# Layer 0's second plan when all tokens are counted, the first convolution's loads in the source's order, and one count for layer 1's last plans

## The chip, the cores and the metric

The kernel runs on one core of a Trainium2 chip. The metric is device time in microseconds (us) of the slowest core, which here is the only one. TensorE, VectorE, ScalarE and GpSimd each run one stream of instructions; SyncE (SP) only issues DMAs. Before the change three runs took 1766.63, 1774.96 and 1779.28 us: a median of 1774.96 us.

## The reference, cut to what matters

Two layers work on an image x of shape [2, 256, 56, 56] in float32. Each adds a token mixer on normalised channels, then a mixture of experts (MoE) on normalised tokens:

```python
# layer 0
x = x + local_attention(_ln_c(x))          # 7 x 7 window, 8 heads
t = _to_tokens(x)                          # 6272 tokens of 256
t = t + moe0(_ln_t(t))                     # returns its own input too
# moe0: probs = softmax(tokens @ router.T); top 2, weights made to sum to 1
#   out = tokens + sum_e combine[:, e] * (gelu(tokens @ w1[e] + b1[e]) @ w2[e] + b2[e])
#   8 experts, 256 -> 256 -> 256
# layer 1
x = x + conv_pair(_ln_c(x))
# conv_pair: out1 = relu(bn(tri_conv(x, w1)))
#            relu(out1 + bn(tri_conv(out1, w2)))
# tri_conv: 3 x 3, 256 -> 256, weights made ternary, centre tap counted twice
t = t + moe1(_ln_t(t))                     # top 2 of 8 experts, 256 -> 512 -> 256
```

Batch norm takes its mean and variance over both images, so the second convolution can't start before the first has ended. Nor can an expert's last tokens be known before the last token is routed.

## The kernel before

**Strips.** The image is cut into 14 strips of 8 rows (448 tokens, held as 112 partitions x 4 tokens). Attention, routing, convolution and the final sums go strip by strip.

**Routing** (`routing`). For each strip `settle` takes the two largest router logits of each token with two calls of `first_max` on VectorE, writes which experts were chosen into `hots`, adds them up in `seen`, and finds each token's place within its expert by two small matmuls (`rk`, the rank). Then GpSimd copies the normalised row `u` of each token to its two places in the DRAM buffer `xs`, by indirect DMAs at L861 (one of 112 rows for each of 4 tokens and 2 choices: 8 per strip). `settle` is a generator: each `yield` ends a step, and the caller runs one step of it beside each step of other work. `gates` makes the final weights of the chosen experts (L880 to L893).

**The plan** (`tiles(part)`, L907 to L996). Expert work is cut into tiles of 256 rows of one expert. Which expert and which rows of `xs` a tile has depends on the routing, so a plan is worked out on the chip: a cast of `seen` (L907), a matmul of it with ones (`counts`, L910), and a chain of short VectorE operations that ends in a table of row addresses and experts (`held`, L996). SP reads this table to start its loads. In layer 0 plan 0, made from the first 10 strips, gives 27 tiles; plan 1, from all strips, the other 29. Layer 1 has plan 0 (27 tiles), plan 1 (14) and plan 2 (23 tiles of 128 rows, mixed in from tile 8 on). Plans 1 and 2 of layer 1 are called one after the other; each makes its own cast and count matmul.

**Experts** (`experts_in_order`). At tile j the code issues: `fetch_rows(j+4)` and `fetch_weights(j+3)` on SP; `turn(j+2)`, the transposes `pt` of the rows (L1060) and their copy (L1064, ScalarE); `first(j+1)`, the first layer `ph` (L1092) and gelu (L1099, ScalarE); `second(j)`, the second layer `py` (L1109), its bias on VectorE (`y`, L1117), and the scatter of y to the result buffer `ys` on GpSimd (L1119); then the callback `at_tile(j)`. Weights have 4 buffers, y has 5, py 2. SP, VectorE, TensorE and ScalarE run in the order in which this code issues (`manual_schedule`); GpSimd's order is left to the scheduler.

**What runs beside layer 0's experts.** The callback is `beside(j)`. It pushes the routing steps of the strips that plan 0 left out (`under_way`), and does the following:

```python
            if j == EARLY[0] - ROWS_AHEAD - 1:      # j == 22
                while under_way:
                    push()
            if len(plans0) > 1:
                for _ in range(4):
                    next(steps, None)               # ternary weights
            elif not under_way:
                routed_all()                        # plan 1 and what follows
```

`routed_all` issues at once: plan 1; all of the gates; the test of whether every strip's tokens fit (`unfit`, a matmul `pf` at L1627, the flag); then it closes attention's pools and opens those of the convolutions in their memory. From the next tile on, four steps per tile of `ternary` prepare the convolutions' weights on VectorE and the rest.

**First convolution** (`combine`, `conv`). For strip i `combine` loads the tokens `x_mid` (L1697; strips 0 to 2 are loaded already at tile 54), loads the expert results `got` (L1159, 896 KB, 2 buffers), adds them with the gates (`add_up`, 8 VectorE operations at L1168), normalises (`xn`), transposes (`pu`), copies into the padded image (ScalarE), and stores the tokens back to `x_mid` (L1712). `conv` makes components of the padded image (`hi` on ScalarE, `lo` on VectorE, `v` on GpSimd) and multiplies by the ternary weights (`pc`, L1752). `combining` calls `combine` for the first three strips ahead of it and two more per pair. The order on all engines is left to the scheduler here, SP's queue included.

Of the kernel before, what the change touches and what calls it, by code (L numbers as in the profile page):

```python
# [20 lines left out]
P = 128  # L21
# [19 lines left out]
E = 8  # L41
# [589 lines left out]
def metaformer(ctx: ExitStack, tc: tile.TileContext, a: dict, out: bass.AP, flag):  # L631
# [98 lines left out]
    def routing(layer, wp, tp, ps):  # L730
# [11 lines left out]
        seen = wp.tile([TT, E], F32, tag="seen", name="seen")  # L742
        nc.vector.memset(seen, 0.0)
        seen_b4 = wp.tile([TT, E], BF16, tag="seen_b4", name="seen_b4")
        counted, sent = [], []
        small_eng = nc.gpsimd if layer == 0 else nc.vector
        rows = {}

# [43 lines left out]
        def settle(strips):  # L792


            n = len(strips) * NTT
            t0 = strips[0] * NTT
            us = [rows.pop(i) for i in strips]
            full, row = [TT, n, E], (TT, n)

            def small(name, shape=(TT, n, E), dt=F32):  # L800
                return tp.tile(list(shape), dt, tag=f"{name}_{n}", name=name, bufs=1)

            def first_max(v, m, hot, at):

                nc.vector.tensor_reduce(m, v, AX.X, ALU.max)
                nc.vector.tensor_tensor(hot, v, bcast(m, 2, full), ALU.is_equal)
                nc.vector.tensor_tensor(hot, hot, bcast(order, 1, full), ALU.mult)
                nc.vector.tensor_reduce(at, hot, AX.X, ALU.min)
                nc.vector.tensor_tensor(
                    hot, bcast(order, 1, full), bcast(at, 2, full), ALU.is_equal  # L810
                )

            lg = lgs[:, t0 : t0 + n, :]
            m = [most[:, j, t0 : t0 + n] for j in range(TOP)]
            hot = small("hot", (TT, TOP, n, E))
            at = small("at", (TT, TOP, n))
            rest = small("rest")
            first_max(lg, m[0], hot[:, 0], at[:, 0])
            for q, u in enumerate(us):
                small_eng.tensor_copy(u[:, :, R_EX], at[:, 0, q * NTT : (q + 1) * NTT])  # L820
            nc.vector.scalar_tensor_tensor(rest, hot[:, 0], NEVER, lg, ALU.mult, ALU.add)
            yield
            first_max(rest, m[1], hot[:, 1], at[:, 1])
            yield

            hots = small("hots", dt=BF16)
            nc.vector.tensor_tensor(hots, hot[:, 0], hot[:, 1], ALU.add)
            seen_b = small("seen_b", (TT, E), BF16)
            nc.vector.tensor_copy(seen_b, seen)
            here = small("here", (TT, E))  # L830
            nc.vector.tensor_reduce(here, hots.rearrange("p n e -> p e n"), AX.X, ALU.add)
            nc.vector.tensor_tensor(seen, seen, here, ALU.add)
            if strips[-1] == FIRST[layer] - 1:
                nc.vector.tensor_copy(seen_b4, seen)
                counted.append(True)
            rk = ps.tile([TT, n, E], F32, tag="aux", name="rk")
            nc.tensor.matmul(rk, before_w, hots, start=True, stop=False)
            nc.tensor.matmul(rk, all_w[:, :TT], bcast(seen_b, 1, full), start=False, stop=n == 1)
            for t in range(n - 1):
                nc.tensor.matmul(  # L840
                    rk[:, t + 1 :, :],
                    all_w[:, :TT],
                    bcast(hots[:, t, :], 1, [TT, n - 1 - t, E]),
                    start=False,
                    stop=t == n - 2,
                )
            yield
            place = small("place")
            nc.vector.tensor_tensor(place, rk, bcast(base_t, 1, full), ALU.add)
            nc.vector.tensor_tensor(hot, hot, bcast(place, 1, [TT, TOP, n, E]), ALU.mult)  # L850
            rowf = small("rowf", (TT, TOP, n))
            nc.vector.tensor_reduce(rowf, hot, AX.X, ALU.add)
            if layer == 1:
                nc.vector.tensor_copy(pos[:, :, t0 : t0 + n], rowf)
            yield
            for t in range(n):
                if layer == 0:

                    nc.vector.tensor_copy(pos[:, :, t0 + t : t0 + t + 1], rowf[:, :, t : t + 1])
                for j in range(TOP):  # L860
                    w = nc.gpsimd.indirect_dma_start(  # L861
                        xs[:, :],
                        bass.IndirectOffsetOnAxis(ap=pos[:, j, t0 + t : t0 + t + 1], axis=0),
                        us[t // NTT][:, t % NTT, :],
                        None,
                    )
                    apart(f"rows{layer}", w)
                    if FIRST[layer] and strips[0] >= FIRST[layer]:

                        disjoint(w, f"late{layer}", f"early{layer}")  # L870
                yield
            sent.extend(strips)

        def gates():
# [20 lines left out]
        def tiles(part, taken=None, halves=False):  # L895
# [2 lines left out]

            sb = seen_b4
            full = part == 0 or part == 1 and halves
            g = P if part == 2 else G
            n = (EARLY[layer], (NFULL if halves else NTILE) - EARLY[layer], NHALF)[part]
            if part:
                sb = wp.tile([TT, E], BF16, tag="seen_all", name="seen_all")
                nc.vector.tensor_copy(sb, seen)  # L907
            tile_n = tile_t[:, :n]
            pc = ps.tile([P, E], F32, tag="aux", name="counts")
            nc.tensor.matmul(pc, all_w, sb, start=True, stop=True)  # L910

            def table(name, *shape):
                return wp.tile([P, *shape], F32, tag=f"{name}{part}", name=name)

            cnt = table("cnt", E)
            nc.vector.tensor_scalar_add(cnt, pc, float(1 - G if full else 0))
            shape = [P, E, NREG * G // g]
            more = wp.tile([P, E * 2 * NREG], F32, tag="more", name="more")
            more = more[:, : E * NREG * G // g].rearrange("p (e n) -> p e n", e=E)
# [241 lines left out]
        )  # L1161
        return y

    def add_up(i, y, wgt, xt):
        for t in range(NTT):
            n = i * NTT + t
            for j in range(TOP):
                nc.vector.scalar_tensor_tensor(  # L1168
                    xt[:, t, :], y[:, t, j, :], wgt[:, j, n : n + 1], xt[:, t, :], ALU.mult, ALU.add
                )  # L1170
# [116 lines left out]
    with ExitStack() as st:  # L1287
# [325 lines left out]
        pads = mid.enter_context(ExitStack())  # L1613
        wq_held = ExitStack()

        def routed_all():

            nonlocal x_all
            plans0.append(tiles0(1, *taken))
            finish(gates0())  # L1620
            unfit = aw.tile([TT, 1], F32, tag="unfit", name="unfit")
            nc.vector.tensor_scalar(fits, fits, float(len(STRIPS)), None, ALU.is_lt)
            nc.vector.tensor_reduce(unfit, fits, AX.X, ALU.add)
            unfit_b = aw.tile([TT, 1], BF16, tag="unfit_b", name="unfit_b")
            nc.vector.tensor_copy(unfit_b, unfit)
            pf = ps.tile([P, 1], F32, tag="aux", name="pf")
            nc.tensor.matmul(pf, all_w, unfit_b, start=True, stop=True)  # L1627
            nc.vector.tensor_scalar_min(flag, pf[0:1, :], 1.0)
            st.close()

            xpool = mid_x.enter_context(tc.tile_pool(name="x", bufs=1, reuse_waits="tile"))
# [28 lines left out]
        def beside(j):  # L1660
            push()
            if j == NTILE - 2:

                for i in range(X_FIRST):
                    nc.sync.dma_start(XT[STRIPS[i]][:TT], x_mid[i])
            if j == EARLY[0] - ROWS_AHEAD - 1:
                while under_way:
                    push()
            if len(plans0) > 1:
                for _ in range(4):  # L1670
                    next(steps, None)
            elif not under_way:
                routed_all()

        experts(0, C, plans0, ys[0], wp0, tp0, ps0, beside)
        for _ in steps:
# [3 lines left out]
    with mid:  # L1680

        with ExitStack() as st:
# [10 lines left out]
            def combine(i):  # L1693

                xt = XT[STRIPS[i]][:TT]
                if i >= X_FIRST:
                    nc.sync.dma_start(xt, x_mid[i])  # L1697
                got = gathered(i, ys[0], tp)
                yield
                add_up(i, got, wgt0, xt)  # L1700
                yield
                rstd, nmr = yield from token_stats(tp, xt, eps6, True)
                xn = tp.tile([TT, NTT, C], F32, tag="xn", name="xn")
                scaled(xn, xt, rstd, nmr)
                yield
                pu = channels(ps, "pu", xn)
                for k in range(KC):
                    nc.scalar.copy(
                        blocks(inner(*STRIPS[i])[:, k]),
                        pu[:, k].rearrange("p (t h w) -> p t h w", h=SR, w=TW),  # L1710
                    )
                nc.sync.dma_start(x_mid[i], xt)  # L1712
# [91 lines left out]
            def combining(n):  # L1804


                if n < 0:
                    for i in range(3):
                        coming.append(combine(i))
                        push_all()  # L1810
                    while coming:
                        push_all()
                    coming.extend(combine(i) for i in (3, 4))
                    push_all()
                    return
# [5 lines left out]
                    coming.append(combine(i))  # L1821
                push_all()

            stats = conv(sums[0], combining)
            scale, shift = affine(stats, bn["g1"], bn["b1"], tp)

            def between(i):
# [269 lines left out]
```

## Time and profile before

The profiled execution took 1913.16 us, its span is 1911.4 us, and its mean granted clock 0.862; the three timed runs were 134 to 147 us shorter. It falls into these stages (from the busy time in stretches, us):

| stage | from | to | TensorE busy | VectorE busy | GpSimd busy | granted clock | DMA share |
|---|---|---|---|---|---|---|---|
| attention | 0 | 555 | 467.0 | 285.9 | 172.1 | 0.89 | 0.28 |
| layer 0 experts | 555 | 888 | 273.8 | 182.0 | 154.1 | 0.88 | 0.74 |
| results, first strips | 888 | 924 | 6.3 | 19.5 | 2.7 | 0.54 | 0.76 |
| first convolution | 924 | 1083 | 153.7 | 139.6 | 49.5 | 0.97 | 0.28 |
| second convolution | 1083 | 1245 | 148.7 | 93.7 | 49.0 | 0.96 | 0.02 |
| layer 1 routing | 1245 | 1451 | 102.3 | 110.5 | 108.3 | 0.52 | 0.39 |
| layer 1 experts | 1451 | 1824 | 373.0 | 61.4 | 96.6 | 1.00 | 0.76 |
| last sums and output | 1824 | 1911 | 42.4 | 47.7 | 6.9 | 0.61 | 0.71 |

Over the whole span:

```profile
PE 1567.3 (82%) x8709; PEld 1226.3 (64%) x8709; DVE 940.3 (49%) x2665; ACT 693.6 (36%) x1344; POOL 639.1 (33%) x665
```

PE is TensorE's matmul, PEld its weight load, DVE VectorE, ACT ScalarE, POOL GpSimd, and x the number of instructions. In lines that list single instructions the first number is the start, the second the duration, and a bracket at the end holds the wait ahead of the instruction and what ended it.

### The profile page before, as it was taken

What the parts mean: (1) busy time and instruction counts of PE and PEld (TensorE: products, weight loads), DVE (VectorE), ACT (ScalarE), POOL (GpSimd) and SP (SyncE); (2) the same over time, 40 slices, a digit from 0 to 9 for tenths busy, and PEclk for the clock granted to TensorE, in tenths of its full rate; (3) what the DMA queues carried; (4) which work ended last, traced back from release to release, by engine and by line L of the source; (5) the groups of instructions that cost most, each with busy time, mean ns of one, the idle gap of its engine ahead of it and who ended that gap; (6) DMA issues with size and microseconds to landing.
All of it is one profiled execution on the core that took longest, in us unless ns stands there. A gap on an engine that the chain in (4) does not pass through costs nothing. (4 is left out here: it accounts for less than half of the span.)

```text
span 1911.4 us, 25968 instructions
## 1 busy us (share of the span) xinstructions
PE 1567.3 (82%) x8709; PEld 1226.3 (64%) x8709; DVE 940.3 (49%) x2665; ACT 693.6 (36%) x1344; POOL 639.1 (33%) x665
## 2 busy tenths in 40 slices
PE   6999797887978876895799899966446999999964
PEld 3555464544547765784688788855335888888852
DVE  4467355444643525784999555576542111111137
ACT  3454332333423423452445442244223333333322
POOL 3012433324143464443133134235553222222210
PEclk9999797888878988998799899955557999999975
DMA  7022333212126777798542000033353787877858
GB/s 236 21 86 78 93 99 97 63 48 69 41 68 220 233 234 252 254 320 257 170 127 67 1 1 1 7 100 103 101 196 111 252 275 265 272 272 273 271 168 304
DMA packets 91887, 291.79 MB, mean 153 GB/s; under 512 B 20487, under 2 KB 35803, under 8 KB 80416
## 3 DMA queue, kind: packets, MB, share of 16 engines
q1 hardware_dynamic: 66736, 231.79, 38.3%
q0 software_dynamic: 21200, 51.82, 7.8%
q10 hardware_dynamic: 3808, 6.42, 1.0%
q8 instruction: 71, 1.16, 0.2%
q14 instruction: 72, 0.59, 0.1%
HBM read 218.51 MB, written 74.20 MB: 153 GB/s over the span
## 5 line engine op out<-in xcount | busy, mean ns | idle before, releaser
L1092 PE MATMUL ph<-ut,w 128*128 128x256 f32 (+1 forms) x1472 | 314.6, 365 | 5.7 <-DMA w<-in_L_experts 4.4
L1109 PE MATMUL py<-w,h 128*128 128x256 f32 x1288 | 299.8, 381 | 0.0
L1117 DVE TENSOR_TENSOR y<-py,w 128x512 f32<-128x512 f32 (+1 forms) x120 | 76.7, 639 | 428.2 <-PE py L1109 371.0
L1092 PEld LDWEIGHTS ph<-ut,w 128*128 128x128 f32 x1472 | 253.9, 197 | 35.1 <-issue 4.5
L1109 PEld LDWEIGHTS py<-w,h 128*128 128x128 f32 x1288 | 245.8, 192 | 33.4 <-DVE y L1117 0.2
L861 POOL DMA_INDIRECT xs<-u,pos x224 | 213.7, 954 | 158.0 <-issue 90.5
L1752 PE MATMUL pc<-hi,wq 128*128 128x448 f32 x672 | 255.8, 381 | 8.7 <-ACT hi L1726 8.7
L1752 PE MATMUL pc<-lo,wq 128*128 128x448 f32 x672 | 255.5, 381 | 1.7 <-DVE lo L1727 1.7
L1119 POOL DMA_INDIRECT ys<-y,dest x136 | 136.3, 1002 | 273.8 <-DVE dest L1067 185.5
L1099 ACT ACTIVATE h<-ph,w 128x256 f32<-128x256 f32 (+1 forms) x368 | 162.4, 447 | 118.7 <-PE ph L1092 74.9
L1448 ACT ACTIVATE ex<-sc 112x476 f32<-112x476 f32 (+3 forms) x224 | 116.8, 570 | 243.3 <-PE sc L1438 168.5
L1064 ACT COPY ut<-pt 128x512 f32<-128x512 f32 (+1 forms) x120 | 65.2, 543 | 314.1 <-PE pt L1060 245.3
L1725 POOL TENSOR_TENSOR v<-pad 128x928 f32<-128x928 f32 (+1 forms) x56 | 98.4, 1764 | 235.0 <-DVE lo L1727 158.3
L1468 DVE TENSOR_TENSOR acc<-av,acc 128x238 f32<-128x238 f32 (+3 forms) x224 | 87.6, 407 | 156.1 <-PE av L1458 71.9
L1458 PE MATMUL av<-ex,vals 112*64 112x238 f32 (+3 forms) x896 | 132.0, 416 | 23.4 <-DVE acc L1468 18.7
L1752 PEld LDWEIGHTS pc<-hi,wq 128*128 128x128 f32 x672 | 129.1, 192 | 23.6 <-ACT hi L1726 9.4
L1752 PEld LDWEIGHTS pc<-lo,wq 128*128 128x128 f32 x672 | 129.6, 193 | 18.2 <-DVE lo L1727 3.7
L1429 PE MATMUL sc<-q_im,keys 32*112 32x238 f32 (+3 forms) x896 | 100.8, 439 | 38.1 <-issue 20.4
L1119 POOL DMA_INDIRECT ys<-y,to x81 | 84.3, 1041 | 127.9 <-DVE dest L1067 65.8
L1168 DVE SCALAR_TENSOR_TENSOR x<-got,wgt,x 112x256 f32<-112x256 f32 x224 | 100.8, 515 | 31.3 <-DMA got<-ys 31.1
L1458 PEld LDWEIGHTS av<-ex,vals 112*64 112x64 f32 x896 | 58.0, 147 | 78.1 <-issue 35.1
L714 POOL TENSOR_TENSOR t_rstd<-t_mv,eps 112x4 f32<-112x4 f32 x26 | 5.3, 203 | 282.7 <-DVE t_mv L703 282.7
(233 smaller groups left out, 2203.4 us busy)
## 6 DMA issues: line engine op xcount, KB each, us to landing
w<-in_L_experts SPq DMA_DIRECT2D x64, 1154.0 KB
w<-in_L_experts SPq DMA_DIRECT2D x56, 641.0 KB
xg<-xs SPq DMA_DIRECT2D x97, 260.0 KB
got<-ys SPq DMA_DIRECT2D x28, 896.0 KB
acc<-in_fresh SPq DMA_DIRECT2D x14, 896.0 KB
xt<-in_x_tok SPq DMA_DIRECT2D x14, 448.0 KB
xr<-in_x_tok SPq DMA_DIRECT2D x14, 448.0 KB
rec<-shares SPq DMA_DIRECT2D x28, 224.0 KB
```

The lines of the kernel that those rows point to most:

```text
L861: w = nc.gpsimd.indirect_dma_start(xs[:, :], bass.IndirectOffsetOnAxis(ap=pos[:, j, t0 + t : t0 + t + 1], axis=0), us[t // NTT][:, t % NTT ...
L1092: nc.tensor.matmul(ph[:, :g], w1[:, k, f * P : (f + 1) * P], d["ut"][:, k, :g], start=k == 0, stop=k == KC - 1,)
L1099: nc.scalar.activation(d["h"][:, f, :g], ph[:, :g], AF.Gelu, bias=b1[:, f : f + 1])
L1109: nc.tensor.matmul(py[:, i, :], d["h"][:, f, i * P : (i + 1) * P], w2[:, f, :], start=f == 0, stop=f == NF - 1,)
L1119: o = nc.gpsimd.indirect_dma_start(ys[:, :], bass.IndirectOffsetOnAxis(ap=d["to"][:, i : i + 1], axis=0), y[:, i, :], None, bounds_check=T ...
L1168: nc.vector.scalar_tensor_tensor(xt[:, t, :], y[:, t, j, :], wgt[:, j, n : n + 1], xt[:, t, :], ALU.mult, ALU.add)
L1429: nc.tensor.matmul(sc[h // 2][:, h % 2, :nq], keys[g][p, c, tx * TT : (tx + 1) * TT], q_im[p, c, r0:r1, c0:c1], start=True, stop=False,)
L1448: nc.scalar.activation(e[:, :, :nq], sc[j][:, :, :nq], AF.Exp, scale=HD**-0.5)
L1458: nc.tensor.matmul(av[VW * i : VW * (i + 1), :nq], vals[g % 3][:, tx, 2 * c + j, 2 * i : 2 * i + 2, :].rearrange("p a d -> p (a d)"), ex[j ...
L1468: nc.vector.tensor_tensor(d, av[:, :nq].rearrange("p (h w) -> p h w", w=c1 - c0), d, ALU.add)
L1725: (nc.gpsimd if u else nc.vector).tensor_tensor(v[:, :, at : at + n, :], *r, op)
L1752: nc.tensor.matmul(pc[:, :NT], wq[:, k, c, dx * C + o * P : dx * C + (o + 1) * P], part[:, k, :, dx : dx + W], start=m == 0, stop=m == 2 * ...
```

## The change

Layer 0. `counted` gets a second entry as soon as the last strip is counted. From then on `beside` runs a new generator, `wind_up`, one piece per tile: plan 1, the pieces of `gates`, the test `unfit`, and `pf` with the flag. When the generator and the routing steps have ended (in the order as built this is tile 20, with the pieces at tiles 15 to 19), `routed_all` only changes the pools. For a strip that is settled alone (`brief`), both maxima and the count are one step, the rank matmuls come one step later, and the row scatters go two tokens (four DMAs) per step.

First convolution. The result loads of the first three strips are issued first, into three buffers. Strip 2's sum takes another way (`away`): eight scaled copies on ScalarE and two additions of 112 x 1024 on GpSimd instead of eight VectorE operations. SP's queue runs in the order of the source, the other engines as before. SP's order, as built, becomes: three `got` loads, three stores of x_mid, x_mid and got of strips 3 and 4, two stores, x_mid and got of strips 5 and 6, and so on.

Layer 1. The counts are copied from PSUM to SBUF (`held_counts`) when plan 0 or plan 1 is made. Plan 2 uses plan 1's copy, without a cast and a count matmul of its own.

```diff
-        counted, sent = [], []
+        counted, sent, held_counts = [], [], []
...
-            yield
+
+            brief = layer == 0 and len(strips) == 1
+            if not brief:
+                yield
             first_max(rest, m[1], hot[:, 1], at[:, 1])
-            yield
+            if not brief:
+                yield
...
                 counted.append(True)
+            if strips[-1] == len(STRIPS) - 1:
+                counted.append(True)
+            if brief:
+                yield
             rk = ps.tile([TT, n, E], F32, tag="aux", name="rk")
...
-                yield
+                if t % 2 or not brief:
+                    yield
...
-            sb = seen_b4
...
-            if part:
-                sb = wp.tile([TT, E], BF16, tag="seen_all", name="seen_all")
-                nc.vector.tensor_copy(sb, seen)
             tile_n = tile_t[:, :n]
-            pc = ps.tile([P, E], F32, tag="aux", name="counts")
-            nc.tensor.matmul(pc, all_w, sb, start=True, stop=True)
+            if part < 2:
+                sb = seen_b4
+                if part:
+                    sb = wp.tile([TT, E], BF16, tag="seen_all", name="seen_all")
+                    nc.vector.tensor_copy(sb, seen)
+                pc = ps.tile([P, E], F32, tag="aux", name="counts")
+                nc.tensor.matmul(pc, all_w, sb, start=True, stop=True)
+                counts = wp.tile([P, E], F32, tag="counts", name="counts")
+                nc.vector.tensor_copy(counts, pc)
+                held_counts[:] = [counts]
...
-            nc.vector.tensor_scalar_add(cnt, pc, float(1 - G if full else 0))
+            nc.vector.tensor_scalar_add(cnt, held_counts[0], float(1 - G if full else 0))
...
-    def add_up(i, y, wgt, xt):
+    def add_up(i, y, wgt, xt, away=False):
+
+        if away:
+            for j in range(TOP):
+                for t in range(NTT):
+                    n = i * NTT + t
+                    nc.scalar.activation(
+                        y[:, t, j, :], y[:, t, j, :], AF.Copy, scale=wgt[:, j, n : n + 1]
+                    )
+                nc.gpsimd.tensor_tensor(xt, xt, y[:, :, j, :], ALU.add)
+            return
...
-        def routed_all():
-
-            nonlocal x_all
+        def wind_up():
+
             plans0.append(tiles0(1, *taken))
-            finish(gates0())
+            yield
+            yield from gates0()
             unfit = aw.tile([TT, 1], F32, tag="unfit", name="unfit")
...
             nc.vector.tensor_copy(unfit_b, unfit)
+            yield
             pf = ps.tile([P, 1], F32, tag="aux", name="pf")
             nc.tensor.matmul(pf, all_w, unfit_b, start=True, stop=True)
             nc.vector.tensor_scalar_min(flag, pf[0:1, :], 1.0)
+
+        winding = wind_up()
+
+        def routed_all():
+
+            nonlocal x_all
             st.close()
...
-            if j == EARLY[0] - ROWS_AHEAD - 1:
+            over = len(counted0) > 1 and next(winding, winding) is winding
+            if x_all is None and (over and not under_way or j == EARLY[0] - ROWS_AHEAD - 1):
                 while under_way:
                     push()
-            if len(plans0) > 1:
+                finish(winding)
+                routed_all()
+            if x_all is not None:
                 for _ in range(4):
                     next(steps, None)
-            elif not under_way:
-                routed_all()
...
-                got = gathered(i, ys[0], tp)
+                got = gathered(i, ys[0], tp, 3)
                 yield
-                add_up(i, got, wgt0, xt)
+                add_up(i, got, wgt0, xt, i == X_FIRST - 1)
...
-                    for i in range(3):
-                        coming.append(combine(i))
+                    first = [combine(i) for i in range(X_FIRST)]
+                    for it in first:
+                        next(it)
+                    for it in first:
+                        coming.append(it)
                         push_all()
...
-            stats = conv(sums[0], combining)
+            with tc.manual_schedule(engines={mybir.EngineType.SP}):
+                stats = conv(sums[0], combining)
```

## The prediction

> **What bounds the kernel now.** I read first the busy time in stretches of 50 us (columns: length; busy us and count of matmul, weight load, VectorE, ScalarE, GpSimd; granted clock; DMA share; GB/s).
>
> ```profile
> 700.00:750.00 50.00, 31.41 (x134) 26.07 (x134) 18.36 (x73) 13.67 (x26) 24.58 (x32) 0.77 0.64 199
> 900.00:950.00 50.00, 31.47 (x135) 25.05 (x136) 42.99 (x117) 21.65 (x42) 3.94 (x2) 0.68 0.55 163
> 1400.00:1450.00 50.00, 15.54 (x86) 14.10 (x85) 17.71 (x89) 6.77 (x14) 30.52 (x33) 0.50 0.42 132
> 1500.00:1550.00 50.00, 50.00 (x274) 44.72 (x273) 8.04 (x26) 18.11 (x42) 13.06 (x14) 1.00 0.78 262
> ```
>
> TensorE sets the pace where it is full (1500 to 1550); what a change can win lies in the three holes above it, and the change touches all three. Next the time line of each hole. Layer 0's second plan, matmul first, then VectorE:
>
> ```profile
> 727.21 1.89 PE L1109 MATMUL py<-w,h 128*128 128x256 f32 x8
> 730.03 0.17 PE L910 MATMUL counts<-seen_all,all_w 112*128 112x8 bf16 x1 [0.93 <-DVE seen_all L907]
> 742.70 0.16 PE L1627 MATMUL pf<-unfit_b,all_w 112*128 112x1 bf16 x1 [12.50 <-DVE unfit_b L1625]
> 742.80 1.09 PE L1060 MATMUL pt<-ident,xg 128*128 128x128 f32 x4
> 729.81 0.17 DVE L907 CAST seen_all<-seen 112x8 bf16<-112x8 f32 x1
> 738.02 0.62 DVE L880 TENSOR_TENSOR lgs<-lgs,most 112x448 f32<-112x448 f32 x1
> 742.49 0.16 DVE L1625 CAST unfit_b<-unfit 112x1 bf16<-112x1 f32 x1
> ```
>
> The reader is to see one tiny matmul (pf) hold all expert tiles for 12.5 us, while VectorE makes the plan (729.8 to 738.0) and the gates (to 742.5). Layer 1's last plans:
>
> ```profile
> 1426.07 0.19 PE L910 MATMUL counts<-seen_all,all_w 112*128 112x8 bf16 x1 [4.49 <-DVE place L849]
> 1450.78 0.19 PE L910 MATMUL counts<-seen_all,all_w 112*128 112x8 bf16 x1 [24.52 <-remote]
> 1450.83 1.95 PE L1060 MATMUL pt<-ident,xg 128*128 128x128 f32 x8
> 1448.05 0.22 DVE L907 CAST seen_all<-seen 112x8 bf16<-112x8 f32 x1
> 1461.70 0.18 DVE L996 TENSOR_TENSOR held<-below,since 128x23 int32<-128x23 f32 x1
> ```
>
> Again one count matmul, in front of all expert work, waits 24.5 us for VectorE to finish plan 1. The chain of waits agrees: a 24.47 us piece ends at 1450.7. Before the first convolution:
>
> ```profile
> 875.46 8.03 SPq L1697 DMA_DIRECT2D x<-x_mid  x6
> 896.51 9.72 SPq L1159 DMA_DIRECT2D got<-ys  x3
> 902.65 3.26 DVE L1168 SCALAR_TENSOR_TENSOR x<-got,wgt,x 112x256 f32<-112x256 f32 x8 [14.67 <-DMA got<-ys]
> 924.17 1.11 PE L1752 MATMUL pc<-hi,wq 128*128 128x448 f32 x2 [0.22 <-ACT hi L1726]
> ```
>
> Nine 448 KB loads stand in front of the expert results; the last scatter of results is issued at 890.35, the first result load only at 896.51.
>
> **What the Trainium skill says.** "DMA: Bandwidth & Descriptors", Anatomy of one DMA: about 2.0 us fixed plus bytes at 436 GB/s. The trace agrees roughly: two 896 KB result loads started together land the first in 6.1 us, against an estimate of 2.0 + 4.2 for both. "TensorE: Matmul & The Clock Gate", Part 1: an idle window of some 3.4 us halves the clock. Agrees: after the 12.5 us hole eight first-layer matmuls take 3.62 us, else 1.89. "ScalarE: Activation LUTs", What ACT_TABLE_LOAD costs: a pass with a pointer operand costs 280 ns + 0.833 per element, overlapping by 93, an estimate of 0.4 us for 256; the trace has 2.06 for four, and I use that.
>
> **Layer 0.** The five pieces of the plan generator fall on tiles 15 to 19; before, all of it followed tile 22. Removed: 12.50 + 0.93 us of waits and 1.7 us of cold clock after them: 15.1. Added: the count matmul now follows tile 15's second layer (free at 681.9) and needs VectorE to finish both maxima of strip 13. From y at 682.6: position casts 0.25, first maximum 1.36, second 1.1, hots to seen 0.6, cast 0.2 (rows at 682.7, 690.4, 701.8): 686.1. That is 4.2 us of wait, with perhaps 0.9 of cold clock. Queued behind it are tile 16's matmuls. The plan's 8.2 us and the count copy's 0.2 then delay y of tile 16 from 689.7 to about 695; two py buffers carry TensorE to about 694, so 0 to 2 us, and weights for tile 20 leave SP by as much later. The gates (4.0) and unfit (0.5) are split over tiles between y's; pf comes a tile after its operand: nothing, with TensorE's 3.9 us per tile as cover, 0.5 each without it. Rank matmuls come a tile after hots: nothing. The same 32 row scatters are issued in fours, so two tiles' ys scatters wait up to 4 x 1.25 = 5 us on GpSimd; five y buffers cover that. SP now meets the flag load and the tap loads three tiles sooner; they wait for the last row scatters, and weights stand behind them: 0 to 3 us. Sum: -15 + 5 + 1 = **-9**; bounds -13 and 0.
>
> **First convolution.** Removed from SP's queue ahead of the results: nine x_mid loads (4 MB). The chain end shows scatter issue to load issue in 3.0 us without such traffic (1841.5 to 1844.5), here 5.2; and the 1.23 us wait for the last weights goes: start T moves from 896.5 to about 893.1. With three got buffers all results load at once, landing at T+6, +9, +12 (estimate, 3 us each). VectorE loses one strip's adds (8 x 0.41 = 3.3). But ScalarE runs six of strip 2's scalings (3.1 us, waiting till T+12) before xn of strip 0, so xn goes from T+14.8 to T+15.1; two more scalings stand before its pad copies. GpSimd's two adds (nearest row 112x1024, 2.43 us each; 3.24 once) end at T+21, stats and xn of strip 2 at T+26, conv at T+27.1, against T+27.7 before. So -4. The cost: SP's third store waits for that second add, and behind it are xt and got of strips 3 and 4, which land near T+28 and T+32 where got 3 was used at T+22.7. VectorE takes their adds ahead of the third component's lo: ready T+42, wanted T+41. +1, and up to +6 if a scatter or store is in the way. Steady state: a result load leaves 16 to 19 us before its use (949.2 to 968), and the added 448 KB takes 1.7, so nothing; TensorE covers (153.7 busy of 159). Sum **-3**; bounds -6 and +4.
>
> **Layer 1.** One cast and one count matmul go; two copies of 0.17 come. TensorE then goes from the count at 1426.3 straight to tile 0, whose rows were loaded from 1405.9 on. It has 24.5 us of work (four first layers, two second) until second layer 2 needs y of tile 0, which stands on VectorE behind plan 2. That ends near 1448.1 + 10.8 (1451.0 to 1461.8) = 1459, y at 1460, TensorE held from 1451 to 1460. Then weights of tile 4 leave SP, 4.7 us by the skill's price, 6.6 at 257 GB/s: first layer 4 at 1467 in place of 1479.2: **-12**. In that stretch VectorE takes 1.40 us between dependent plan operations (1431.9 to 1436.1), in layer 0 0.2 to 0.4. I can't say why; at the quick pace plan 1 takes 8.5 us and the win is 8.5. Bounds -15 and -6.
>
> **Sum.** -9 - 3 - 12 = -24 against the profiled 1913.2 us: 1889. The median, 1775, is 138 us shorter, so some waits are shorter in it; I take -21: **1754 us**.
>
> **Rivals.** *Layer 0 gives nothing*: GpSimd issues 62 indirect DMAs from 647 to 737, 79 us of 90; if it sets the pace, the stall only hid its backlog. Against it: ys follows y by one tile at 720. Only layer 1 is left: 1765. *More than that*: all low bounds, -34: 1741. *Slower*: SP's fixed order in the first convolution. VectorE is 99% busy from 945 to 1045, so a result that lands after VectorE reaches it is not made up. If a store held back each of five pairs by 8 us, 40 - 21 = +19: 1794. It decides when a load leaves less than about 7 us ahead of its add; the slack shown speaks against it. *Not as said*: the plan may still wait for the last count; the built order puts it at tile 15, so little.
>
> **Numbers.** Forecast 0.62 (1746 to 1766), layer 0 nothing 0.20, more 0.08, slower 0.10. 1% is 17.7 us, about what a measurement of this kernel can tell from no change: faster means under 1757, three quarters of the forecast, all of "more" and a tenth of the second: 0.56. Slower 0.09, within 0.35. Range 1738 to 1772: it leaves out the slower case and the second's upper end.
>
> **What would show it.** No wait over 5 us at pf and 4 us at counts near tile 15; got load within 3.5 us of the last scatter, conv 3 us sooner after expert work's end; pt of layer 1 within 1 us of its count, then one 9 us hole at second layer 2. Wrong: a longer hole between tiles 16 and 24, VectorE waits for got after 945, or layer 1's hole whole.

## The result, and the profile after

The changed kernel takes 1762.99 us (median of 19 runs, 1750.18 to 1770.85), the kernel before 1773.85 us (19 runs, 1756.27 to 1784.68). The ratio is 0.9953, with a 95% interval of 0.993 to 0.9976: a gain of 8.3 us (4 to 12; the two medians alone are 10.9 apart), where 21 were forecast and 1754 us given. The profiled execution of after has a span of 1767.6 us.

On some occasions every version of this kernel takes about 1900 to 1920 us instead of about 1770, the profile shown before (1913 us) is of that kind while the times beside it are not, and so below profiles and times of one kind are compared with each other. The kernel before was therefore profiled again, with a span of 1777.4 us (first experiment), and that profile is what "before" means from here on, unless the first is named.

The busy time in stretches of 50 us (columns as in the prediction) where the three holes lie now:

```profile
650.00:700.00 50.00, 32.14 (x147) 27.04 (x148) 27.33 (x65) 18.14 (x43) 21.97 (x30) 0.83 0.68 236
800.00:850.00 50.00, 23.36 (x95) 17.81 (x93) 25.93 (x69) 19.50 (x39) 12.47 (x10) 0.66 0.62 172
1300.00:1350.00 50.00, 48.04 (x234) 42.21 (x235) 20.76 (x88) 21.86 (x40) 37.82 (x41) 0.93 0.79 264
```

and the same stretches before, from the second profile:

```profile
650.00:700.00 50.00, 33.11 (x143) 27.66 (x143) 27.43 (x86) 17.45 (x42) 22.59 (x31) 0.80 0.63 230
800.00:850.00 50.00, 18.57 (x77) 13.19 (x76) 25.75 (x77) 15.30 (x29) 7.78 (x8) 0.64 0.81 228
1300.00:1350.00 50.00, 39.33 (x190) 34.41 (x190) 21.50 (x96) 17.38 (x31) 36.67 (x39) 0.81 0.70 224
```

The hole of layer 1 is closed (TensorE busy for 48.04 of 50 us, before 39.33). The one in layer 0's experts is still there: 32.14, before 33.11. The time line of the three after the change, matmuls first, then VectorE; a line begins with start and duration in us:

```profile
619.66 0.17 PE L920 MATMUL counts<-seen_all,all_w 112*128 112x8 bf16 x1 [4.30 <-DVE seen_all L918]
638.47 0.16 PE L1651 MATMUL pf<-unfit_b,all_w 112*128 112x1 bf16 x1 [0.30 <-DVE unfit_b L1648]
662.54 1.11 PE L1073 MATMUL pt<-ident,xg 128*128 128x128 f32 x4 [16.00 <-ACT ut L1077]
841.80 1.12 PE L1783 MATMUL pc<-hi,wq 128*128 128x448 f32 x2 [0.22 <-ACT hi L1757]
1302.96 0.19 PE L920 MATMUL counts<-seen_all,all_w 112*128 112x8 bf16 x1 [1.25 <-DVE seen_all L918]
1303.01 1.95 PE L1073 MATMUL pt<-ident,xg 128*128 128x128 f32 x8
1313.44 3.62 PE L1122 MATMUL py<-w,h 128*128 128x256 f32 x16
1316.66 0.18 DVE L1009 TENSOR_TENSOR held<-below,since 128x23 int32<-128x23 f32 x1
1317.15 0.69 DVE L1130 TENSOR_TENSOR y<-py,w 128x512 f32<-128x512 f32 x1
```

The wait at `pf` is gone (0.30 us), and the count matmul waits 4.30 us: both as forecast. But 24 us after `pf` the experts' transposes wait 16.00 us. In layer 1 the transposes follow their count without a gap; the last plan is ready at 1316.66 and y of tile 0 comes right behind it, soon enough that nothing waits: the hole expected at tile 2's second layer does not exist.

The start of the first convolution is seen on GpSimd and SP:

```profile
811.98 0.97 POOL L1132 DMA_INDIRECT ys<-y,to  x1 [0.30 <-issue]
814.21 1.44 SPq L1172 DMA_DIRECT2D got<-ys  x3
```

The result loads begin 2.2 us after the last scatter of results is issued, and the first `pc` at 841.80 follows 27.6 us later.

Where the new 16 us come from is told by the engines in the same stretch, GpSimd first, then SP's queue, ScalarE and VectorE. The "taps" below are the convolutions' weights as they are loaded, before they are made ternary:

```profile
654.55 0.94 POOL L869 DMA_INDIRECT xs<-u,pos  x1 [0.30 <-issue]
655.79 0.99 POOL L1132 DMA_INDIRECT ys<-y,dest  x1 [0.30 <-issue]
657.28 0.82 SPq L1243 DMA_DIRECT2D x<-in_L_conv_w_flat  x2
661.29 0.63 ACT L1255 ACTIVATE low<-x 128x512 f32<-128x512 f32 x1 [19.86 <-DMA x<-in_L_conv_w_flat]
661.92 0.56 ACT L1077 COPY ut<-pt 128x512 f32<-128x512 f32 x1
661.29 0.69 DVE L1250 TENSOR_REDUCE st<-x 128x1 f32<-128x512 f32 x1 [17.91 <-DMA x<-in_L_conv_w_flat]
```

and by the list of SP's waits in this window (columns: waited for, us in total, times, longest):

```profile
SPq L1243 <- DMA xs<-u,pos: 16.8, 4, 13.2
```

The last row scatter is issued at 654.55. SP, at the first load of taps, waits 13.2 us for it: the taps go into memory of attention's pools, and the trace names the row scatters as what SP waits for. On ScalarE the first operation on the taps (`low`) is ordered ahead of the next tile's `ut`, and waits 19.86 us; `ut` runs at 661.92 and releases TensorE. VectorE waits at its own first operation on the taps (`st`) for 17.91 us, with the experts' next y behind it.

Stages of the two profiles and of single experiments, in us, each between the starts of two groups of matmuls (layer 0's experts: first `ph` to the `py` of the last two tiles, 16 matmuls in one line; start: from there to the first `pc`; then to the second convolution's first; layer 1: the last `pc` to the `py` of the last four tiles, 32 matmuls in one line, with the routing):

| kernel | layer 0's experts | start of convolution 1 | convolution 1 | layer 1 to its last py |
|---|---|---|---|---|
| before, again | 283.8 | 40.6 | 171.7 | 533.6 |
| after | 283.2 | 36.5 | 172.1 | 527.4 |
| layer 1's part alone | 284.5 | 43.1 | 171.8 | 527.3 |
| layer 0's part alone | 289.5 | 40.7 | 171.2 | 533.4 |
| convolution's part alone | 279.4 | 36.7 | 172.0 | 532.9 |
| after, taps from tile 24 | 275.9 | 36.8 | 172.1 | 526.6 |

In the first column kernels with the same code differ by up to 6.3 us (283.2 and 289.5 with layer 0's part; 283.8, 284.5 and 279.4 without it), so there a single profile shows nothing smaller. The last column is steadier: 532.9 to 533.6 with two counts, 526.6 to 527.4 with one.

### The profile page after: what moved, and what is told of

Same layout as the page of the kernel before. It is cut to its first block, busy times and chain, and to the rows that moved or that the text cites. A ratio compares the mean times of both kernels' runs of the same rounds, so it can differ in the third digit from the quotient of the medians.

```text
span 1767.6 us, 25976 instructions
## 1 busy us (share of the span) xinstructions
PE 1531.5 (87%) x8708; PEld 1212.7 (69%) x8708; DVE 946.4 (54%) x2660; ACT 696.5 (39%) x1352; POOL 652.2 (37%) x667
## 4 chain that ended last, share of the span: by engine, by line
PE 64%; DVE 15%; DMA 11%; issue 4%; POOL 2%; ACT 2%; SPq 1%; POOLq 0%; DVEq 0%; ACTq 0%
PE ph L1105 15%; PE py L1122 14%; PE pc L1783 11%; PE av L1481 4%; PE pw L1550 3%; PE pj L1404 3%; PE sc L1452 3%; PE pv L1426 3%; PE pt L1073 3%; DVE x L1191 3%; DVE oc L1537 2%; DMA out<-o_out 2%; DMA got<-ys 2%; PE pl L778 2%; POOL xs L869 2%
## 5 line engine op out<-in xcount | busy, mean ns | idle before, releaser
L1105 PE MATMUL ph<-ut,w 128*128 128x256 f32 (+1 forms) x1472 | 310.9, 363 | 6.4 <-DMA w<-in_L_experts 6.4
L869 POOL DMA_INDIRECT xs<-u,pos x224 | 219.2, 978 | 130.1 <-issue 59.2
L1481 PE MATMUL av<-ex,vals 112*64 112x238 f32 (+3 forms) x896 | 121.7, 393 | 17.2 <-DVE acc L1491 16.9
L1191 DVE SCALAR_TENSOR_TENSOR x<-got,wgt,x 112x256 f32<-112x256 f32 x216 | 99.1, 527 | 34.2 <-DMA got<-ys 33.9
L1757 ACT CAST hi<-v 128x928 fp32r<-128x928 f32 x56 | 54.2, 967 | 122.9 <-PE pc L1783 114.0
L1073 PE MATMUL pt<-ident,xg 128*128 128x128 f32 x434 | 70.2, 282 | 25.1 <-ACT ut L1077 18.2
```

The costliest lines, as they stand in the source:

```text
L869: w = nc.gpsimd.indirect_dma_start(xs[:, :], bass.IndirectOffsetOnAxis(ap=pos[:, j, t0 + t : t0 + t + 1], axis=0), us[t // NTT][:, t % NTT ...
L1073: nc.tensor.transpose(pt[:, k, i * P : (i + 1) * P], d["xg"][:, i, k * P : (k + 1) * P], ident)
L1105: nc.tensor.matmul(ph[:, :g], w1[:, k, f * P : (f + 1) * P], d["ut"][:, k, :g], start=k == 0, stop=k == KC - 1,)
L1191: nc.vector.scalar_tensor_tensor(xt[:, t, :], y[:, t, j, :], wgt[:, j, n : n + 1], xt[:, t, :], ALU.mult, ALU.add)
L1481: nc.tensor.matmul(av[VW * i : VW * (i + 1), :nq], vals[g % 3][:, tx, 2 * c + j, 2 * i : 2 * i + 2, :].rearrange("p a d -> p (a d)"), ex[j ...
```

## The experiments

**The kernel before, profiled again** (no edit).

> The kernel before, profiled once more, because its first profiled execution was 138 us above the median. Theory A (the 24.5 us hole ahead of layer 1's experts belonged to that execution): the count matmul of the second last plan waits about 5 us, since plan 1 takes 5 us on VectorE in the profile after. Theory B (the hole is the kernel's own): 20 us or more. Both expect the pf wait of about 12 us in layer 0 and the first convolution about 33 us after the last scatter of results is issued.

Its span is 1777.4 us. The matmuls:

```profile
648.08 0.17 PE L910 MATMUL counts<-seen_all,all_w 112*128 112x8 bf16 x1 [0.93 <-DVE seen_all L907]
660.64 0.16 PE L1627 MATMUL pf<-unfit_b,all_w 112*128 112x1 bf16 x1 [12.40 <-DVE unfit_b L1625]
1313.64 0.19 PE L910 MATMUL counts<-seen_all,all_w 112*128 112x8 bf16 x1 [5.91 <-DVE seen_all L907]
```

and the start of the first convolution, on GpSimd, SP and TensorE:

```profile
813.25 0.97 POOL L1119 DMA_INDIRECT ys<-y,to  x1 [0.30 <-issue]
820.08 9.71 SPq L1159 DMA_DIRECT2D got<-ys  x3
847.16 1.11 PE L1752 MATMUL pc<-hi,wq 128*128 128x448 f32 x2 [0.22 <-ACT hi L1726]
```

`pf` waits what it waited in the first profile. The hole ahead of layer 1's experts is 5.91 us, not 24.5. From the last scatter (813.25) to the first `pc` (847.16) it is 33.9 us, after 29.8. Theory A.

**Each part alone.** Three kernels, each the kernel before with one section of the diff, nothing else.

> Only the counts kept in SBUF, so one count for layer 1's last plans. Theory A: 5 us faster (ratio 0.997), because plan 1 takes 5 us at VectorE's usual pace. Theory B (the prediction's own size): 12 us faster (0.993). Theory C (the wait moves to the second layer of tile 2): no change (1.000).

> Only layer 0's part: plan and gates in pieces, brief settling, ternary weights from tile 20. Theory A (the tap loads, now met earlier, hold SP behind the last row scatters, and ScalarE and VectorE hold the taps' first operations ahead of the experts' own): a wait of 10 to 18 us on TensorE about two tiles after the pieces end, and no gain in all, ratio 0.998 to 1.004. Theory B (prediction): 9 us faster, 0.995, no wait over 5 us there.

> Only the first convolution's part: result loads first, three buffers, strip 2's sum on ScalarE and GpSimd, SP in the source's order. Theory A: 3 us faster (0.998), the first convolution about 4 us sooner after the last scatter of results. Theory B (SP's order costs as much in the pairs that follow): same or up to 5 us slower (1.000 to 1.003).

| part alone | ratio to before | 95% interval | in us of 1769.8 |
|---|---|---|---|
| layer 1 | 0.9966 | 0.9943 to 0.9989 | -6.0 |
| layer 0 | 0.9997 | 0.9973 to 1.0022 | -0.5 |
| first convolution | 0.997 | 0.9951 to 0.9989 | -5.3 |

The sum, -11.8, agrees with the -8.3 of the whole within the intervals. Layer 1's part wins the 5.9 us of its hole (6.3 us in the stages, 533.6 against 527.3). Layer 0's part shows no gain, and its profile has the same three matmuls as the whole change:

```profile
614.43 0.17 PE L919 MATMUL counts<-seen_all,all_w 112*128 112x8 bf16 x1 [4.26 <-DVE seen_all L916]
633.27 0.16 PE L1637 MATMUL pf<-unfit_b,all_w 112*128 112x1 bf16 x1 [0.29 <-DVE unfit_b L1634]
657.40 1.11 PE L1069 MATMUL pt<-ident,xg 128*128 128x128 f32 x4 [16.05 <-ACT ut L1073]
```

Removed at `pf` 12.1 us, added at the count 3.3 and at `pt` 16.0. So the wait belongs to layer 0's part. (By these three alone the part would be 7 us slower; over the whole stage the time without a matmul grows by 5.1 us, from 35.9 to 41.0, and the timed runs show neither gain nor loss.) In the convolution's part SP's first result load is issued at 800.94 after a last scatter at 798.71: 2.2 us, where before it was 6.8 (813.25 to 820.08). That is the gain; from that load to the first `pc` it takes 27.7 us, before 27.1.

**The ternary weights later.** In the changed kernel the pools change, and with them the taps begin, at tile 24 or 22 instead of 20:

```diff
-            if x_all is None and (over and not under_way or j == EARLY[0] - ROWS_AHEAD - 1):
+            if j == EARLY[0] - ROWS_AHEAD - 1:
                 while under_way:
                     push()
                 finish(winding)
+            if x_all is None and j == 24:
                 routed_all()
```

Most of these runs fell on occasions with before at 1921 to 1923 us; only one, with tile 24, had before at 1769, the kind on which the 16 us were seen.

> The whole change, but the pools change and the ternary weights start at tile 24, four tiles later. Theory A (the 16 us wait is the tap loads standing behind the row scatters): the wait is gone, since the last row scatter is issued by then, and the time falls 15 to 17 us below the changed kernel, ratio to before 0.985 to 0.987. Theory B (GpSimd's backlog of scatters sets the pace of the experts there, whatever stands on SP): a wait of 8 us or more returns at pt, py or ph around the same tiles, on y or its buffers, and the ratio stays at 0.991 to 0.995.

> The whole change with the ternary weights from tile 22, the tile of the kernel before. Theory A: the first tap load is met two tiles (7.8 us) later, and SP's wait for row scatters shrinks from 13.2 us to about 5, TensorE's from 16.0 to about 8. Theory B: the wait keeps its 16 us.

> The changed kernel once more, on the same chip as the next three, so that each can be set beside it. Ratio to before 0.993 to 0.998 as measured before, if before takes about 1770 us there. If before takes about 1920 us: 0.993 to 1.000, with the wait at the tap loads changed in size, since the row scatters end at another tile.

> Ternary weights from tile 24. Theory A (the 16 us wait is the tap loads standing behind the row scatters): the wait of 16 us at pt is gone and the time is 13 to 17 us below the changed kernel, 0.985 to 0.988 of before. Theory B (GpSimd's backlog sets the pace whatever stands on SP): the waits return within the next six tiles, and the time is within 4 us of the changed kernel.

> Ternary weights from tile 22. Theory A: SP meets the first tap load two tiles later, so the wait at pt shrinks from 16 us by 7.8 to about 8 us, and the time lies halfway between the changed kernel and the run with tile 24. Theory B: the wait and the time are those of the changed kernel.

> Ternary weights from tile 24. Where before takes about 1770 us: Theory A (tap loads behind the row scatters cost the changed kernel 16 us there): no wait over 5 us at pt around tiles 20 to 24, ratio 0.985 to 0.988, a stage of layer 0's experts of 268 to 272 us instead of 283. Theory B (GpSimd's backlog sets the pace): the stage stays at 278 us or more, ratio 0.992 to 0.996. Where before takes about 1920 us: 0.991 to 0.995, as in the two runs before.

> Layer 0's part alone, with ternary weights from tile 24. Where before takes about 1770 us: Theory A: 12 to 15 us faster than before (0.992 to 0.993), where layer 0's part with tile 20 gave 0.9997. Theory B: 0.997 to 1.000. Where before takes about 1920 us: 0.996 to 1.000.

> Ternary weights from tile 24. Where before takes about 1770 us: Theory A (tap loads behind the row scatters cost the changed kernel 16 us there): no wait over 5 us at pt around tiles 20 to 24, a stage of layer 0's experts of 268 to 272 us instead of 283, ratio 0.985 to 0.988. Theory B (the backlog of scatters sets the pace): the stage stays at 278 us or more, ratio 0.992 to 0.996. Where before takes about 1920 us: 0.991 to 0.997, as in the three runs before.

> The changed kernel on the same chip as the last run with tile 24 (0.9941 of before, stage of layer 0's experts 275.9 us). Theory A (the early tap loads cost it 16 us less what the row loads of tile 27 would wait anyway, 9.4 us): stage 281 to 284 us, wait of 16 us at pt, ratio 0.996 to 0.998. Theory B (no cost, the difference was noise): stage within 3 us of 275.9, ratio 0.993 to 0.995.

| kernel | before, us | ratio (95% interval), one entry per occasion |
|---|---|---|
| changed kernel | 1922 to 1923 | 0.9943 (0.9921 to 0.9965), 0.9924 (0.9897 to 0.9952) |
| taps from 22 | 1922 to 1923 | 0.9944 (0.9923 to 0.9964); one more run took 1911.7 us |
| taps from 24 | 1921 to 1923 | 0.993 (0.9908 to 0.9952), 0.9927 (0.9906 to 0.9948), 0.9958 (0.9938 to 0.9978) |
| layer 0's part, taps from 24 | 1921 | 0.9978 (0.9961 to 0.9995) |
| taps from 24 | 1769 | 0.9941 (0.9917 to 0.9965) |

Theory A forecast 0.985 to 0.988 for tile 24; no run came near it. The rows at 1921 to 1923 can't decide it, though. In the changed kernel's two profiles there, SP waits for the row scatters at the taps for 1.2 us in one and not at all in the other, so there was no such wait to remove. (`pt` waits for `ut` there all the same, up to 10.4 and 7.8 us in the changed kernel, 8.0 and 6.6 with tile 22, 6.7 to 6.8 with tile 24.) At 1769 tile 24 gave 0.9941, on another occasion than the changed kernel's own 0.9953; the changed kernel's last run, meant to stand beside it, met 1922 again. The profile at 1769 says why so little was won. The matmuls:

```profile
615.72 0.17 PE L920 MATMUL counts<-seen_all,all_w 112*128 112x8 bf16 x1 [4.30 <-DVE seen_all L918]
634.03 0.16 PE L1651 MATMUL pf<-unfit_b,all_w 112*128 112x1 bf16 x1 [0.50 <-DVE unfit_b L1648]
656.92 0.99 PE L1073 MATMUL pt<-ident,xg 128*128 128x128 f32 x4 [3.13 <-DMA xg<-xs]
659.96 3.78 PE L1105 MATMUL ph<-ut,w 128*128 128x256 f32 x8 [2.05 <-DMA w<-in_L_experts]
```

and the waits in the window from 580 to 720, of SP and then of TensorE:

```profile
SPq L1052 <- DMA xs<-u,pos: 9.4, 1, 9.4
```

```profile
PE ph L1105 <- DMA w<-in_L_experts: 6.3, 3, 2.4
PE counts L920 <- DVE seen_all L918: 4.3, 1, 4.3
PE pt L1073 <- DMA xg<-xs: 3.1, 1, 3.1
```

The 16 us wait is gone, so the early taps did make it. But SP still stands 9.4 us, now at L1052: the row load of tile 27, the first tile of plan 1, which may hold rows of any strip and needs every row scattered. Weights of the next tiles are behind it in SP's order, and TensorE waits for rows and weights instead. The kernel before has the same wait of SP in this window, at its own row load:

```profile
SPq L1039 <- DMA xs<-u,pos: 9.6, 1, 9.6
```

Added up from the time line over layer 0's experts, the time without a matmul is 35.9 us before, 38.5 after and 34.6 with tile 24: the waits changed their names more than their sum. The stage was 7.3 us shorter in this one profile (275.9 against 283.2), hardly more than the 6.3 by which two profiles with the same code there differ, and the timed ratios overlap, so a gain of tile 24 over the change isn't shown. No run sent the row scatters off sooner; that they alone hold the rest is argued from these waits.

**The plan one tile later**, together with tile 24 (`next(winding, None)` ahead of `push()` in `beside`), so that the last count has a tile's time.

> As the run with tile 24, and the plan's pieces one tile later, so that the last strip's maxima and count have a tile to themselves before the count matmul. Theory A (the 4.3 us wait at the count is VectorE finishing both maxima): it falls below 1 us, and the time 3 to 5 us below the run with tile 24 alone. Theory B: the wait only moves to the y that stands behind the plan on VectorE; no change between the two.

The ratio is 0.9932 (0.9908 to 0.9955), beside 0.993 for tile 24 alone on the same occasion (before at 1922). The count matmul waits 7.54 us, where tile 24 alone has 4.26 there, and it waits for the y that comes ahead on VectorE. The wait moved, theory B.

**Strip 2's sum on VectorE**, with the changed kernel and with tile 24:

```diff
-                add_up(i, got, wgt0, xt, i == X_FIRST - 1)
+                add_up(i, got, wgt0, xt)
```

> The whole change, but strip 2's sum stays on VectorE. Theory A (the start of the first convolution is set by the landing of the last result load and what follows it, and by moving the adds little is won): from the last scatter to the first convolution 30 to 33 us, where the changed kernel takes 29.8; ratio to before 0.995 to 0.997. Theory B (the detour costs more than it frees, since strip 0's xn waits on ScalarE behind six scalings): 28 us or less, ratio 0.994 or lower.

> As the run with tile 24, and strip 2's sum on VectorE. Theory A (the detour over ScalarE and GpSimd costs, as the run without it showed with 28.3 us from the last scatter to the first convolution against 29.8): 1 to 2 us below the run with tile 24. Theory B (the difference is noise of one profile): no difference, and the first convolution 29 us or more after the last scatter.

> As the run with tile 24, and strip 2's sum on VectorE: 1 to 2 us less, from the last scatter to the first convolution 28 to 28.5 us against 29.8. Theory B: no difference.

> Ternary weights from tile 24 and strip 2's sum on VectorE, on the same chip as before: stage of layer 0's experts 274 to 278 us, 34.4 to 35.1 us from the last second layer to the first convolution (36.8 with the detour), ratio 0.992 to 0.994. If the detour is worth its cost: 36 us or more there, 0.994 to 0.996.

The last two tiles' `py` and the first `pc`, with tile 24: first with the detour over ScalarE and GpSimd, then with the sum on VectorE, on the same occasion:

```profile
886.62 3.62 PE L1122 MATMUL py<-w,h 128*128 128x256 f32 x16
923.35 1.11 PE L1784 MATMUL pc<-hi,wq 128*128 128x448 f32 x2 [0.22 <-ACT hi L1758]
```

```profile
873.98 3.62 PE L1122 MATMUL py<-w,h 128*128 128x256 f32 x16
909.01 1.12 PE L1784 MATMUL pc<-hi,wq 128*128 128x448 f32 x2 [0.22 <-ACT hi L1758]
```

That is 36.7 us against 35.0. In the four profiles without the detour the start takes 35.1, 35.0, 34.8 and 35.2 us (the 34.4 in the last expectation is a misreading of the third). Eight profiles with it at about the same total time (the changed kernel twice, the runs with tile 22 or 24, the later plan) give 36.3 to 36.9. So the detour costs about 1.6 us at the place where it was to save some. In the timed runs this is too small to be told. Ratios without the detour: 0.9924 (0.9894 to 0.9953) with the taps as in the change; with tile 24 0.9913 (0.989 to 0.9936), 0.9923 (0.99 to 0.9947) and 0.992 (0.989 to 0.9949). Two of these have a neighbour on the same occasion that differs by the detour alone, and lie below it, but not clearly: 0.9913 beside 0.9927, and 0.9923 beside 0.9958. Tile 24 without the detour has the lowest ratio measured, but no version is shown to beat the changed kernel.

## Why the prediction was right or wrong

**Layer 0, forecast -9, measured -0.5 (from 4.8 faster to 3.9 slower): a term mis-sized.** The steps on the waits hold: 12.4 us at `pf` went to 0.3, and the count matmul waits 4.30 (4.2 forecast). What failed is the sentence "SP now meets the flag load and the tap loads three tiles sooner; they wait for the last row scatters, and weights stand behind them: 0 to 3 us". The wait was seen, but only SP's queue behind it was priced. The first operations on the taps stand in ScalarE's and VectorE's order too, ahead of the experts' `ut` and y, and there a 13.2 us wait of SP became 16.0 us on TensorE. Behind it lies what the rival "layer 0 gives nothing" said: plan 1's row load waits for GpSimd's row scatters, before (9.6 us on SP) as with the later taps (9.4 us), and the stall at `pf` covered part of that backlog. That the rival's price for the whole, 1765 us, came nearest to 1763 is partly luck: it counted on layer 1 alone for some 10 us, and that came half from layer 1 and half from the first convolution.

**Layer 1, forecast -12, measured -6.0: the hole's size.** The mechanism is right: a count matmul less, the transposes 0.05 us behind the other. The term was read from an execution in which that matmul waited 24.5 us; in the second profile it waits 5.91, and plan 2 ends early enough that no hole of 9 us follows. The prediction named the slow pace and gave 8.5 for the quick one, itself too high, yet put -12 into the sum, and took only 3 us off the whole for an execution 138 us above the median.

**First convolution, forecast -3, measured -5.3 (1.9 to 8.7 faster): right in size, partly by luck.** The "-4" for the start is met: that stage is 4.1 us shorter. But its parts were others. The first load comes 4.6 us sooner after the last scatter (2.2 against 6.8), where 3.4 were forecast; the 5.2 and 3.0 us that the prediction compared begin at different points of a scatter, and from its start to the load's its own profile has 6.2. From that load to the first `pc` it takes 0.5 us longer (27.6 against 27.1), where the detour was to save 0.6. SP's fixed order adds 0.4 us to the convolution (172.1 against 171.7), less than two profiles can tell apart (171.2 to 172.1 in the table). The sign of being wrong, VectorE waiting for `got` in the convolution, did come, three times and 5.3 us in all where before had none; the stage grew by no more than those 0.4 us.

**Two prices.** The Trainium skill's page "DMA: Bandwidth & Descriptors" gives the figure used, in "Anatomy of one DMA", for DMAs that GpSimd issues; the prediction used it for SP's loads. What supports it there is the prediction's own pair of result loads, 6.1 us against 6.2. For the six scalings on ScalarE the prediction set aside the estimate of 0.4 us each, made from the skill's page "ScalarE: Activation LUTs" ("What ACT_TABLE_LOAD costs"), and took 3.1 us for all, from slower passes in the trace; measured are 2.50 us, 0.42 each, so the estimate was nearer.

**Sum.** 9 and 12 became 0.5 and 6.0, 14.5 us less; the first convolution gave 2.3 us more than its 3. That is the whole difference between -24 and the -11.8 of the parts.

## What to carry to other kernels

When a stall is taken away, look for the next in-order point where a queue meets the same late event: here the row scatters held SP at the tap loads, and without these at the row load of tile 27. An operation that starts earlier takes its place in the order of every engine that it uses, not only on the queue of its loads. And a wait's size is to be taken from an execution that is as long as the timed runs: in a profile 8% longer one wait was the same (12.5 and 12.4 us) and another four times as long (24.5 and 5.9). Stages are to be measured between the same two instructions: a time line that is asked for piece by piece cuts the last group of matmuls in different places.

## What the runs showed of the hardware

Between the two profiles of before, of 1911.4 and 1777.4 us, only the stages in which rows are routed differ by more than 3 us: up to the first expert matmul 583.1 against 522.7 us, layer 0's experts 300.6 against 283.8, layer 1's routing, up to its first expert matmul, 212.7 against 152.7. The two convolutions and layer 1's experts take the same time within 1 us (171.8 and 171.7, 143.9 and 143.9, 386.7 and 387.7). In the longer ones ScalarE and VectorE have waits for which the profile names no releaser ("remote"). Of such waits over 1 us the first profile of before has 15 on VectorE (105 us in all) and 16 on ScalarE (121 us); the second, the changed kernel at 1767.6 and tile 24 at 1753.1 have none. GpSimd is busy with row scatters for 57% and 58% of their time, and for 11% of the whole span. In the changed kernel at 1900.6 us (matmul, GpSimd, ScalarE, VectorE):

```profile
681.80 1.89 PE L1122 MATMUL py<-w,h 128*128 128x256 f32 x8
...
683.38 0.95 POOL L869 DMA_INDIRECT xs<-u,pos  x1 [0.30 <-ACT ut L1077]
...
689.67 0.94 POOL L869 DMA_INDIRECT xs<-u,pos  x1 [0.30 <-issue]
688.35 0.47 ACT L1112 ACTIVATE h<-ph,w 128x256 f32<-128x256 f32 x1 [2.34 <-remote]
692.61 0.69 DVE L1130 TENSOR_TENSOR y<-py,w 128x512 f32<-128x512 f32 x1 [11.74 <-remote]
```

Its `py` ends at 683.7, y starts at 692.61, 2.0 us after the last of six scatters. The scatters themselves take the same 0.94 us (median) at both speeds. There no gain of layer 1's part can be seen either: the last `pc` to the last four tiles' `py` takes 594.3 us on average of the twelve profiles with one count (588.4 to 598.1), and 592.7 and 597.9 in the two with two. Those two wait 24.5 and 27.4 us at the last count matmul; with one count TensorE begins sooner and waits in most of them in the experts' first layers instead, for instance

```profile
1430.30 5.33 PE L1105 MATMUL ph<-ut,w 128*128 128x256 f32 x16 [10.07 <-issue]
1447.69 5.17 PE L1105 MATMUL ph<-ut,w 128*128 128x256 f32 x16 [11.63 <-ACT h L1112]
```

in the third run of tile 24, whose last row scatter is issued at 1440.6. What holds the engines then, and why it happens on some occasions only, stays open; no run tested it. It isn't the chip alone: the same one took about 1770 us for the parts run alone and about 1920 us two hours later.
